# More landing time for the DMAs of two layers in a list-scheduled four-layer graph kernel

## The chip, the cores and the metric

The kernel runs on one core of a Trainium2 chip. The metric is the device time of one execution in microseconds (us). An instruction "record" is one entry of the trace. PE is the matmul engine, PEld its weight load, DVE the vector engine, ACT the scalar engine, POOL GpSimd, and SP the engine that issues nearly all DMAs, from one queue that is worked through in order.

## The reference, cut to what matters

There are 128 graphs of 128 nodes, with 512 features a node, all in fp32. Four different graph layers follow each other, each with a residual and a layer norm.

```python
def reference(x, adj, ...):                       # x (128,128,512), adj (128,128,128)
    # layer 0: attention-like transition, used twice, three weights
    e = leaky_relu(sj[:, None, :] + si[:, :, None] + ab[0])
    alpha = adj * exp(e)
    transition = alpha / (alpha.sum(-1) + 1e-12)
    for k in range(3):
        H = H + Xk @ Wk[k] + bk[k]
        Xk = einsum('bij,bjd->bid', transition, Xk)
    x = layernorm(x + relu(H))
    # layer 1: hypergraph convolution 512 -> 1024 -> 512
    Hm = (adj != 0); w = adj[:, 0, :]             # first row of adj as weights
    conv = lambda x, W, b: Dn * (Hm @ (Be * (Hm^T @ (x @ W^T)))) + b
    y = conv(layer_norm(relu(conv(x, W1, b1))) * gamma + beta, W2, b2)
    x = layernorm(x + (y + x))
    # layer 2: tanh attention over adj; layer 3: 8-head attention, scores scaled by adj + adj
    x = layernorm(x + layer2(x, adj))
    x = layernorm(x + layer3(x, adj))
    return x
```

## The kernel before

The kernel writes no instruction directly. Every operation is first recorded in a `Plan`, with an estimated duration, the operations it depends on and the buffers it needs. A list scheduler (`order`) then plays the whole program through with those estimates, gives each operation a start and each tile a buffer, and `emit` issues the operations in the order of these starts. On the chip each engine takes its instructions strictly in that order and waits at semaphores, so the estimates decide the order and the buffers, and nothing else.

```python
WHEN0 = (-3.0, -1.6, -1.0, 0, 0)                  # when a stage of layer 0 is due, in periods
WHEN1 = (-3.0, -2.3, -1.6, -1.1, .2, .6)          # the same for layer 1; the first entry: its loads
LATENCY = ((0, 205, 215, 255, 300), (225, 120, 110, 200, 200), (160, 145, 140, 200, 200),
           (110, 140, 100, 105, 200), (2300, 2300, 2300, 2300, 2300))   # from engine (row) to engine, ns
ISSUE, BEGIN = 450, 1000
# (cut)
class Plan:
    def add(self, engine, call, name, args, kw):
        moved = 0
        if name == "dma_start":
            run, parts = kw.pop("run", D), kw.pop("parts", P)
            n = next(a for a in args if isinstance(a, View) and a.tile.kind != "dram").idx.size
            moved = 1.1 * parts * max(n // run, 1) * (8 + .038 * 4 * min(run, n)) / 16
        ns = estimate(engine, name, out, rest, kw) * self.share      # ISSUE for a DMA
        if self.group is not None and self.group < len(self.ops):    # "together": one op of several calls
            op = self.ops[self.group]
            op[1].append((call, args, kw)); op[2] += ns; op[7] += moved
        else:
            op = [engine, [(call, args, kw)], ns, (self.key, k), set(), [], shares_port(...), moved]
        # (cut: which earlier operations it depends on)

    def order(self, urgent=None):
        # (cut: ready lists; an operation is picked by rank among those that can start soonest)
            start[k] = t
            free[e] = end = t + o[2]
            if o[7]:                                                 # a DMA: one pipe for all of them
                end = pipe = max(pipe, t + BEGIN) + o[7]
            # (cut)
                    slots[tile.kind].append((end + max(LATENCY[SP if o[7] else e]), place[tile]))
            for j in after[k]:
                come[j] = max(come[j], end + LATENCY[SP if o[7] else e][f])

    def deadlines(self, start):                                      # gives the ranks of a second pass
        # (cut)
                ns, e = (BEGIN + ops[d][7], SP) if ops[d][7] else (ops[d][2], ops[d][0])
                last[d] = min(last[d], by - ns - LATENCY[e][ops[k][0]])
```

Two helpers make groups of small DMAs. `from_dram` loads a tile in blocks that are later turned by the vector engine's 32 by 32 transposes, and `through_dram` writes a tile to device memory and gives back a function that reads it again in another layout.

```python
    def from_dram(src, kind):                     # layer 0: x, as "four"; layer 1: adj, as "sq"
        for j in range(nj):                       # the two graphs of a pair
            with plan.together():
                for k in range(4):
                    sp.dma_start(t[k * Q:(k + 1) * Q, :, j], ..., run=n // 4, parts=Q)   # 32 partitions

    def through_dram(src, name, in_order=True):   # "e" in layer 0, "h" in layer 1, "x" before layer 3
        for j in range(nj):
            with plan.together():
                for m in range(4):
                    sp.dma_start(part(d, ..., j), src[m * Q:(m + 1) * Q, j], run=nw, parts=Q)
        def load(): ...                           # one DMA back
```

Layer 1, for four graphs at a time (its first stages and the hidden layer):

```python
    def layer1(i0):
        loaded = [(load_rows(x1d[i // U]), from_dram(adj[i:i + U], sq)) for i, in each(both)]
        yield                                     # stage 0 above is due at WHEN1[0]
        for (_, ab), in each(loaded):             # stage 1, due at WHEN1[1]
            AT = sq()
            turned(AT, ab)                        # DVE transpose of the adjacency rows
            HT = sq(); cnt = col(U)
            for b in range(U):
                ve.tensor_scalar(HT[:, b], AT[:, b], 0.0, None, op0=OP.not_equal, op1=OP.add, accum_out=...)
        # (cut: HB on POOL, K = H B H^T on PE, x1 K, the left operands of the fast matrix products)
        twice(left, WT["w1"], ...)                # two levels of Strassen: PE into banks, DVE adds
        for r, i in enumerate(both):              # DVE scale and bias, ACT relu and norm, then:
            loads.append(through_dram(h[r][b]..., f"h{i + b}"))
        # (cut: reload h turned, second product, residual, norm, store to x2d)
```

The driver:

```python
    plan.key = -9
    prepare0()
    layer(layer0, 0, WHEN0, size=2)
    # (cut: prepare1, the weights of layer 1)
    layer(layer1, n + LAG1, WHEN1, size=2)
    # (cut: prepare2, prepare_w, prepare3, the weights of layers 2 and 3)
    layer(layer23, 2 * n + LAG1 + LAG2, WHEN2, ramp, size=2)
    plan.emit(places)
```

Of the kernel before, what the change touches and what calls it, by code (L numbers as in the profile page):

```python
# [34 lines left out]

WHEN0 = (-3.0, -1.6, -1.0, 0, 0)
WHENT = (.8, 2.1), (2.0, 3.1)
WHEN1 = (-3.0, -2.3, -1.6, -1.1, .2, .6)
STEP1 = .22
WHENH, WHENW, WHENG = (2.4, 3.0), (2.9, 3.6), (3.6, 4.3)  # L40
WHEN2 = (-2.4, -2.0, -1.45, -1.15, -.7, .3, .5, 2)
WHENV, WHENS, WHENP, WHENO = (.9, 1.9), (2.2, 3.2), (3, 4), (3.5, 4.5)
LAG1, LAG2 = 1, 1.5
SOFT = .2
RAMP = 0, 0, .05, 4

# [10 lines left out]
PE, DVE, ACT, POOL, SP = range(5)  # L57

LATENCY = ((0, 205, 215, 255, 300), (225, 120, 110, 200, 200), (160, 145, 140, 200, 200), (110, 140, 100, 105, 200),
           (2300, 2300, 2300, 2300, 2300))  # L60
# [11 lines left out]
class Tile:  # L72
# [3 lines left out]
    def __init__(self, kind, ap=None):  # L76
        self.kind, self.ap = kind, ap
        self.reads, self.writes = [], []
# [65 lines left out]
def shares_port(engine, name, args, kw):  # L144

    if engine == POOL:
        return name != "memset"
    views = [a for a in args if isinstance(a, View)]
    sbuf = [a for a in views[1:] if a.tile.kind not in PSUM and a.idx.size > 1]
    if engine != DVE or not sbuf:  # L150
        return False
    if name in ("tensor_scalar", "tensor_copy"):
        return "accum_out" not in kw and views[0].idx.size > 1
    return len(sbuf) > 1


def overlap(a, b):

    if a[1] < b[0] or b[1] < a[0]:
        return False  # L160
    if a[3] is None and b[3] is None:
        return True
    one, two = (np.arange(e[0], e[1] + 1) if e[3] is None else e[3] for e in (a, b))
    return np.intersect1d(one, two, assume_unique=True).size > 0


class Plan:


    def __init__(self, slots, later):  # L170
        self.slots = slots
        self.later = later
        self.key = 0
        self.group = None
        self.share = 1
        self.ops = []

    def engine(self, number, real):
# [7 lines left out]
    def add(self, engine, call, name, args, kw):  # L186
        out, rest = args[0], args[1:]
# [5 lines that stand above are left out]
        ns = estimate(engine, name, out, rest, kw) * self.share  # L193
        if self.group is not None and self.group < len(self.ops):
            k = self.group
            op = self.ops[k]
            op[1].append((call, args, kw))
            op[2] += ns
            op[7] += moved
        else:  # L200
            k = len(self.ops)
            op = [engine, [(call, args, kw)], ns, (self.key, k), set(), [], shares_port(engine, name, args, kw), moved]
            self.ops.append(op)
        reads = [a for n, a in [*enumerate(rest), *kw.items()] if isinstance(a, View) and n != "accum_out"]
        writes = [a for a in (out, kw.get("accum_out")) if isinstance(a, View)]
        for v, is_write in [(v, False) for v in reads] + [(v, True) for v in writes]:
            t = v.tile
            if t.kind == "free":
                continue
            if t.kind not in ("fixed", "dram") and t not in op[5]:  # L210
                op[5].append(t)
            lo, hi = int(v.idx.min()), int(v.idx.max())
            whole = v.idx.size > hi - lo
            entry = (lo, hi, k, None if whole else np.unique(v.idx))
            op[4].update(e[2] for e in t.writes if overlap(e, entry))
            if is_write:
                op[4].update(e[2] for e in t.reads if overlap(e, entry))
                if whole:
                    t.reads = [e for e in t.reads if e[0] < lo or e[1] > hi]
                    t.writes = [e for e in t.writes if e[0] < lo or e[1] > hi]  # L220
                t.writes.append(entry)
            else:
                t.reads.append(entry)
        op[4].discard(k)
# [7 lines left out]
    def order(self, urgent=None):  # L232


        ops = self.ops
# [11 lines left out]
        slots = {kind: [(0, i) for i in range(m)] for kind, m in self.slots.items()}  # L247
        place = {}
# [17 lines left out]
        come, free, start = [0.0] * n, [0.0] * 5, [0.0] * n  # L266
# [37 lines left out]
        while count < n:  # L304
            t, e = min((b[0], e) for e, b in enumerate(best) if b)
            k = best[e][1]
            o = ops[k]
            stale = {e}
            for tile in o[5]:
                if tile not in place:  # L310
                    s, l = slots[tile.kind], line[tile.kind]
                    at = min(s)
                    s.remove(at)
                    place[tile] = at[1]
                    l.remove(tile)
                    settle(tile.kind)
                    stale = set(range(5))
            del ready[e][k]
            start[k] = t
            free[e] = end = t + o[2]  # L320
            if o[7]:
                end = pipe = max(pipe, t + BEGIN) + o[7]
            if e == PE and o[3][0] > reached:
                reached = o[3][0]
                stale.add(SP)
            if o[6]:
                port[DVE + POOL - e] = end
                stale.add(DVE + POOL - e)
            count += 1
            for tile in o[5]:  # L330
                todo[tile] -= 1
                if not todo[tile]:
                    slots[tile.kind].append((end + max(LATENCY[SP if o[7] else e]), place[tile]))
                    settle(tile.kind)
                    stale = set(range(5))
            for j in after[k]:
                f = ops[j][0]
                come[j] = max(come[j], end + LATENCY[SP if o[7] else e][f])
                left[j] -= 1
                if not left[j]:  # L340
                    ready[f][j] = come[j]
                    stale.add(f)
            for f in stale:
                best[f] = look(f)
        return start, place, max(free)

    def deadlines(self, start):

        ops = self.ops
        last = [s + 20000 for s in start]  # L350
        for k in sorted(range(len(ops)), key=lambda k: -start[k]):
            for d in ops[k][4]:
                by = start[k] if ops[k][0] == PE else last[k]
                ns, e = (BEGIN + ops[d][7], SP) if ops[d][7] else (ops[d][2], ops[d][0])
                last[d] = min(last[d], by - ns - LATENCY[e][ops[k][0]])
        return last

    def emit(self, places, rounds=2):
# [19 lines left out]
def kernel(  # L378
# [21 lines left out]
    for kind, (n, _) in spans.items():  # L400
        places[kind] = [first[:, at(kind, k):at(kind, k) + SIZE[kind]] for k in range(n)]
        if kind != "w7":
            for k in range(n):
# [3 lines left out]
    slots = {"w7": 7, "out": OUTS, "q7": 0, "q3": 0, "h": 0, "w28": 0, "sq": SQS, "col": COLS, "row": ROWS, "bank": 6, "t0": 1, "t1": 1,  # L407
             "four": BUFS, "row1": 1, "k": KS}
# [16 lines left out]
    plan = Plan(slots, later)  # L425
# [831 lines left out]
    def attention(i0, A, qT, kT, v, x3d, base, r):  # L1257
# [7 lines left out]
        with plan.together(.65):  # L1265
            for b in range(U):
                for i in range(C):
                    for r2 in range(2):
                        pe.matmul(ps[b][r2][:, i * P:(i + 1) * P],
                                  qT[r2 * HD:(r2 + 1) * HD, b, i],  # L1270
                                  kT[r2 * HD:(r2 + 1) * HD, b, i], start=True, stop=True)
        plan.key += SOFT
        for b in range(U):
# [54 lines left out]
    def layer(job, start, when, ramp=lambda k: 0, size=1):  # L1328
        for k in range(0, n, size):
            stages = job(k * U)  # L1330
            for w in when:
                plan.key = start + k + w + ramp(k)
                if start + k + w == when[0]:
                    plan.key = -9.5
                next(stages, None)

    def ramp(k):
        return -RAMP[0] * max(RAMP[1] - k, 0) - RAMP[2] * max(k + RAMP[3] + 1 - n, 0)

    plan.key = -9  # L1340
    prepare0()
    layer(layer0, 0, WHEN0, size=2)
    for job, start, step in ((prepare1, n - 5, .5),):
        plan.key = start
        for k, _ in enumerate(job()):
            plan.key = start + step * (k + 1)
    layer(layer1, n + LAG1, WHEN1, size=2)
    for job, start, step in ((prepare2, 2 * n + LAG1 - .3, .1), (prepare_w, 2 * n + LAG1, 0),
                             (prepare3, 2 * n + LAG1 + 2, .1)):
        plan.key = start  # L1350
        for k, _ in enumerate(job()):
            plan.key = start + step * (k + 1)
    layer(layer23, 2 * n + LAG1 + LAG2, WHEN2, ramp, size=2)
    ctx.enter_context(tc.manual_schedule())
    plan.emit(places)
# [28 lines left out]
```

## Time and profile before

Three runs took 5480.13 us (median; 5480.02 to 5481.23). The profiled execution spans 5477.4 us at a granted matmul clock of 0.994.

| what | value |
|---|---|
| DMA issues of the program | 786374 packets on SP's queue, 759.71 MB |
| mean rate | 140 GB/s, 45.3% of the 16 DMA engines' span |
| x rows of layer 0, 64 KB each | 512 issues, median 2.0 us from issue to landing |
| adjacency rows of layer 1, 16 KB each | 512 issues, median 2.7 us |
| h blocks stored, 128 KB each | 496 issues from one buffer, median 2.4 us |
| h read back, 512 KB each | 87 issues into one kind of buffer, median 4.6 us |

Every operation is recorded by one line of the program (L369), so lines tell nothing here, and groups are told apart by their tiles: `four`, `out`, `first`, `sq`, `col` and `ks` are buffers in the on-chip memory, `bank` and `t` are matmul banks, and `h`, `e`, `x1d`, `x2d` and `K` are scratch in device memory. Layer 0 fills the trace up to about 1300 us, layer 1 from there to about 3100 us, and layers 2 and 3 the rest.

### The profile page before, as it was taken

Reading aid. Unit: us, or ns where it says so; the run is one execution under the profiler, and the core shown is the slowest. Engines: PE = TensorE matmul, PEld = TensorE weight load, DVE = VectorE, ACT = ScalarE, POOL = GpSimd, SP = SyncE. Lnnn points to the kernel's source line nnn. Section 1 sums busy time; section 2 is a strip of 40 time slices with the busy share of each in tenths; the row PEclk is TensorE's granted clock in tenths of the full one; section 3 lists DMA queues with packets and bytes.
Section 4 is the critical chain, followed back from the end, with each engine's and each line's share of the span. In section 5 each row is a group of like instructions: output and inputs, shape, how many; then the busy total and the mean of one; then the engine's idle time right before and its main releaser. Section 6 shows DMA issues by size and latency. Waiting matters only on the chain.

```text
span 5477.4 us, 94041 instructions
## 1 busy us (share of the span) xinstructions
PE 5346.1 (98%) x29145; PEld 4258.7 (78%) x29145; DVE 4549.0 (83%) x11553; ACT 2397.3 (44%) x6479; POOL 4037.1 (74%) x4835
## 2 busy tenths in 40 slices
PE   7999999999999999999999999999999999999998
PEld 4555555555788888888888789899999999999987
DVE  6888887878998899998999978777778777877876
ACT  2444343444443434443434345444455445445444
POOL 6666666666777777777777567777777777777776
PEclk8999999999999999999999999999999999999999
DMA  3333333334554544544454545554454555555553
GB/s 92 98 100 98 104 94 107 93 98 126 153 152 144 155 141 151 155 144 151 149 151 148 161 132 164 160 163 153 161 162 155 162 164 152 161 165 156 161 155 119
DMA packets 788381, 768.35 MB, mean 140 GB/s; under 512 B 264859, under 2 KB 592547, under 8 KB 787878
## 3 DMA queue, kind: packets, MB, share of 16 engines
q1 hardware_dynamic: 786374, 759.71, 45.3%
q8 instruction: 231, 3.78, 0.3%
q10 hardware_dynamic: 1504, 2.62, 0.2%
q14 instruction: 272, 2.23, 0.1%
HBM read 435.83 MB, written 326.24 MB: 139 GB/s over the span
## 4 chain that ended last, share of the span: by engine, by line
PE 56%; DVE 7%; DMA 3%; POOL 2%; issue 1%; ACT 1%; SPq 1%; DVEq 0%; POOLq 0%; ACTq 0%
PE bank L369 42%; PE t L369 14%; DVE first L369 2%; DVE col L369 2%; DVE out L369 1%; DVE four L369 1%; POOL out L369 1%; SPq L369 1%; DMA out<-h 1%; DMA h<-first 1%; DMA out<-x3d 1%; POOL first L369 0%; DMA first<-x3d 0%; ACT first L369 0%; DVE junk L369 0%
## 5 line engine op out<-in xcount | busy, mean ns | idle before, releaser
L369 PE MATMUL bank<-first,four 128*128 128x386 f32 (+3 forms) x5176 | 1438.1, 431 | 32.5 <-DVE out L369 14.2
L369 PEld LDWEIGHTS bank<-first,four 128*128 128x128 f32 (+2 forms) x5176 | 846.3, 187 | 588.6 <-DVE out L369 141.5
L369 DVE TENSOR_TENSOR out<-bank,out 128x386 f32<-128x386 f32 (+1 forms) x1884 | 926.6, 509 | 275.5 <-PE bank L369 215.6
L369 POOL TENSOR_TENSOR out<-out 128x256 f32<-128x256 f32 (+3 forms) x482 | 548.6, 1149 | 297.3 <-DVE out L369 214.0
L369 POOL TENSOR_TENSOR col<-col,neghalf 128x1 f32<-128x1 f32 x640 | 378.8, 597 | 375.6 <-DVE col L369 373.9
L369 DVE TENSOR_TENSOR first<-bank,first 128x256 f32<-128x256 f32 x1362 | 542.1, 412 | 129.6 <-PE bank L369 99.0
L369 PE MATMUL bank<-first,out 128*128 128x256 f32 (+2 forms) x2560 | 623.4, 381 | 25.7 <-DVE first L369 10.1
L369 PEld LDWEIGHTS bank<-first,out 128*128 128x128 f32 (+1 forms) x2560 | 469.4, 190 | 127.3 <-DVE first L369 30.6
L369 PE MATMUL bank<-four,out 128*128 128x256 f32 (+2 forms) x2118 | 538.1, 376 | 2.9 <-DVE col L369 1.4
L369 DVE TENSOR_TENSOR four<-bank,four 128x256 f32<-128x256 f32 x818 | 337.7, 417 | 142.9 <-PE bank L369 128.3
L369 PE MATMUL bank<-out,first 128*128 128x128 f32 (+2 forms) x2840 | 427.8, 290 | 2.2 <-DVE out L369 1.2
L369 ACT COPY out<-bank 128x258 f32<-128x258 f32 (+2 forms) x555 | 236.6, 431 | 419.7 <-PE bank L369 378.6
L369 PEld LDWEIGHTS bank<-four,out 128*128 128x128 f32 (+2 forms) x2118 | 369.7, 189 | 59.1 <-issue 8.4
L369 PEld LDWEIGHTS bank<-out,first 128*128 128x128 f32 (+1 forms) x2840 | 374.4, 188 | 26.0 <-DVE four L369 2.8
L369 ACT ACTIVATE col<-col,col 128x1 f32<-128x1 f32 x640 | 183.2, 292 | 456.2 <-POOL col L369 390.1
L369 POOL TENSOR_TENSOR four<-four,four 128x256 f32<-128x256 f32 (+2 forms) x395 | 329.0, 837 | 13.0 <-DVE four L369 3.2
L369 ACT COPY t<-out 128x512 f32<-128x512 f32 x256 | 150.2, 591 | 421.9 <-DVE four L369 217.6
L369 POOL TENSOR_TENSOR first<-first 128x512 f32<-128x512 f32 (+3 forms) x196 | 232.2, 1197 | 110.3 <-DVE first L369 73.9
L369 POOL TENSOR_TENSOR out<-out,out 128x256 f32<-128x256 f32 (+2 forms) x286 | 288.2, 1011 | 9.3 <-DVE four L369 4.4
L369 POOL TENSOR_TENSOR four<-four 128x256 f32<-128x256 f32 (+2 forms) x331 | 244.3, 754 | 67.6 <-DVE four L369 38.3
L369 POOL TENSOR_SCALAR sq<-sq,col 128x128 f32<-128x128 f32 x256 | 160.5, 636 | 153.4 <-DVE col L369 149.0
L369 DVE BATCH_NORM_STATS2 col<-first 128x6 f32<-128x512 f32 x370 | 245.5, 681 | 27.2 <-ACT first L369 25.4
(406 smaller groups left out, 12715.2 us busy)
## 6 DMA issues: line engine op xcount, KB each, us to landing
h<-first SPq DMA_DIRECT2D x496, 128.0 KB, 2.4
out<-x1d SPq DMA_DIRECT2D x88, 512.0 KB, 4.3
out<-h SPq DMA_DIRECT2D x87, 512.0 KB, 4.6
four<-in_x_dram SPq DMA_DIRECT2D x512, 64.0 KB, 2.0
four<-in_x_dram SPq DMA_DIRECT2D x62, 512.0 KB, 3.5
x1d<-four SPq DMA_DIRECT2D x62, 512.0 KB, 2.7
first<-S SPq DMA_DIRECT2D x61, 512.0 KB, 4.4
out<-S SPq DMA_DIRECT2D x50, 512.0 KB, 4.4
```

What stands on the lines that cost most here:

```text
L369: call(*map(real, args), **{n: real(a) for n, a in kw.items()})
```

## The change

The order is made with longer DMAs. An operation that moves data gets a margin, which is added in the plan to its end: to the time at which its readers can start, and to the time at which its buffers come free. The margin is 1.5 us for what layer 0 records, 3.0 us for what is recorded from layer 1 on up to the weights of layers 2 and 3, and nothing for layers 2 and 3 themselves. Besides, the first stage of layer 1 (x rows and adjacency rows) is due 3.5 periods ahead instead of 3.0. No operation is added or removed, and no duration of a compute operation is changed; order and buffers are what comes out differently.

```diff
-WHEN1 = (-3.0, -2.3, -1.6, -1.1, .2, .6)
+WHEN1 = (-3.5, -2.3, -1.6, -1.1, .2, .6)
+MARGIN = 1500, 3000, 0
...
-            op = [engine, [(call, args, kw)], ns, (self.key, k), set(), [], shares_port(engine, name, args, kw), moved]
+            op = [engine, [(call, args, kw)], ns, (self.key, k), set(), [], shares_port(engine, name, args, kw), moved,
+                  self.margin if moved else 0]
...
-                    slots[tile.kind].append((end + max(LATENCY[SP if o[7] else e]), place[tile]))
+                    slots[tile.kind].append((end + o[8] + max(LATENCY[SP if o[7] else e]), place[tile]))
...
-                come[j] = max(come[j], end + LATENCY[SP if o[7] else e][f])
+                come[j] = max(come[j], end + o[8] + LATENCY[SP if o[7] else e][f])
...
-                last[d] = min(last[d], by - ns - LATENCY[e][ops[k][0]])
+                last[d] = min(last[d], by - ns - ops[d][8] - LATENCY[e][ops[k][0]])
...
+    plan.margin = MARGIN[0]
     layer(layer0, 0, WHEN0, size=2)
...
+    plan.margin = MARGIN[1]
     layer(layer1, n + LAG1, WHEN1, size=2)
...
+    plan.margin = MARGIN[2]
     layer(layer23, 2 * n + LAG1 + LAG2, WHEN2, ramp, size=2)
```

More of the change, by code (lines that the diff above doesn't have):

```diff
@@ L175, in __init__ @@
         self.share = 1
+        self.margin = 0
         self.ops = []
```

## The prediction, made before the changed kernel ran

> **What bounds the kernel now.** I read the busy times of the page first, then a table by stretches, then the waits of one stretch, and last the timeline around one wait.
>
> ```profile
> PE 5346.1 (98%) x29145; PEld 4258.7 (78%) x29145; DVE 4549.0 (83%) x11553; ACT 2397.3 (44%) x6479; POOL 4037.1 (74%) x4835
> ```
>
> PE, the matmul engine, is busy for 98% of the span: 5477.4 - 5346.1 = 131 us are all that is left idle on it. The change adds and removes no matmul, so it can only move these 131 us. Where they lie is seen in the table by stretches (borders in us, length, busy us and records of each engine, granted clock, share of the DMA engines, GB/s):
>
> ```profile
> 0.00:137.00 137.00, 108.12 (x315) 60.65 (x316) 92.48 (x178) 38.00 (x87) 90.59 (x105) 0.89 0.34 92
> 137.00:1150.00 1013.00, 1009.54 (x3003) 544.02 (x3001) 824.38 (x2112) 415.97 (x967) 682.03 (x814) 1.00 0.34 100
> 1150.00:1450.00 300.00, 276.38 (x1004) 171.92 (x1003) 254.73 (x639) 121.17 (x266) 202.08 (x247) 0.98 0.40 118
> 1450.00:3100.00 1650.00, 1620.85 (x7735) 1363.18 (x7734) 1493.65 (x3698) 673.27 (x1269) 1272.99 (x1482) 1.00 0.50 151
> 3100.00:3300.00 200.00, 180.51 (x1118) 156.23 (x1116) 162.90 (x395) 76.66 (x228) 119.23 (x145) 0.97 0.46 142
> 3300.00:5300.00 2000.00, 1994.59 (x14830) 1822.44 (x14829) 1597.30 (x4237) 987.91 (x3366) 1550.89 (x1912) 1.00 0.51 160
> 5300.00:5477.00 177.00, 156.10 (x1153) 140.25 (x1151) 123.57 (x301) 84.31 (x298) 119.30 (x135) 0.96 0.39 127
> ```
>
> Length minus the first busy figure is PE's idle time: 28.9 us in the start, 3.5 in layer 0, 23.6 where layer 0 passes into layer 1, 29.2 in layer 1, 19.5 where layers 2 and 3 begin, 5.4 in them, 20.9 in the tail. Layer 0 is full. Layer 1 is the one steady stretch with something to gain, and there DVE is busy for 1493.65 of 1650 us, 91%, so a DVE that is held up for a microsecond soon holds up PE.
>
> What PE waits for in layer 1 (total us, times, longest), and then DVE's waits for DMAs in the same stretch:
>
> ```profile
> PE bank L369 <- DVE col L369: 10.4, 11, 1.8
> PE bank L369 <- DVE first L369: 7.5, 17, 1.0
> PE t L369 <- DVE col L369: 3.6, 3, 1.8
> PE t L369 <- DVE first L369: 2.7, 7, 0.7
> ```
>
> ```profile
> DVE sq L369 <- DMA sq<-in_adj_dram: 8.6, 9, 1.4
> DVE out L369 <- DMA out<-x1d: 0.3, 1, 0.3
> ```
>
> PE waits for DVE, not for a DMA. DVE waits for one kind of DMA, the adjacency rows, nine times, 8.6 us in all. The timeline shows one of the nine from the issue to the damage: first SP's queue, then DVE, then PE.
>
> ```profile
> 1845.64 0.44 SPq L369 DMA_DIRECT2D out<-h  x1
> 1846.14 5.38 SPq L369 DMA_DIRECT2D sq<-in_adj_dram  x8
> ```
>
> ```profile
> 1851.64 0.17 DVE L369 BATCH_NORM_AGGREGATE col<-col 128x2 f32<-128x6 f32 x1
> 1853.21 0.45 DVE L369 STREAM_TRANSPOSE sq<-sq 128x256 f32<-128x256 f32 x1 [1.39 <-DMA sq<-in_adj_dram]
> ```
>
> ```profile
> 1854.02 0.70 PE L369 MATMUL t<-first,out 128*128 128x256 f32 x2 [1.13 <-DVE col L369]
> ```
>
> The eight small DMAs of one pair take SP 5.38 us to issue, behind a 512 KB reload of h. They are there at 1853.2, 7.1 us after the first issue. DVE stands for 1.39 us at the transpose, in front of the additions that free the banks, and PE stands for 1.13 us. The wait names the statistics (col) as PE's releaser; the root is the DMA.
>
> **What the Trainium skill says.** The page "DMA: Bandwidth & Descriptors", section "Anatomy of one DMA — SWDGE (gpsimd) path", says that DMA engines do not wait on semaphores and that any wait happens on the issuing sequencer before dispatch. The trace agrees for SP's queue too: in layer 1 it stands 571.8 us in 120 waits for ACT's results in the buffer `first` (the h that is stored), and all that stands behind is issued later. "Perfetto Trace Analysis", section "Per-instruction lifecycle: what the profiler-reported window actually captures", says that the window of a DMA on the issuing engine leaves out the movement of the data. It agrees: an adjacency DMA shows a median of 0.43 us on SP and lands 2.8 us after its issue. "Rules for kernel authors" of the DMA page advises to issue early and to wait late, which is what a margin asks of the order; that it helps here no run has shown yet. "Identifying the Most-Contended Engine" of the trace page warns that matmul busy time says little of the distance to the roofline. That is so, but PE's pace when it is not idle is constant here (243 records in each 50 us of layer 1 that is full), so that its idle time does say what a new order can win.
>
> **The change part by part.**
>
> (1) Adjacency rows of layer 1. The old plan takes a group of four such DMAs as 0.45 us of issue each and lets the data flow from 1.0 us after the group's start: 1.1 x 32 x 4 x (8 + .038 x 128) / 16 = 113 ns each, 0.9 us for eight, then 2.3 us latency. That is 4.2 us from the start to the transpose. In the trace eight issues alone take 8 x 0.43 = 3.4 us (5.38 in the case above) and the last lands at least 1.5 us, at the median 2.8 us later: 4.9 to 8.2 us. The plan is thus 1 to 4 us short, and the margin of 3.0 us makes it 7.2 us. Listing both programs in their order of issue, I counted the matmul calls between the start of a group of these loads and the transpose that reads them: before, 9 at least, 10 at the tenth percentile, 15 at the median; after, 13, 29 and 55. A call is two records, 50 us / 121.5 = 0.41 us. (Of the 40 calls more, the start half a period sooner is most: 64 pairs in 1300 to 3100 us make 28 us a period, half of it 14 us or 34 calls; the margin's 3 us are 7.) So the distance goes from 3.7, 4.1 and 6.2 us to 5.3, 12 and 23 us. All but the very nearest loads land well in time, and most of the 8.6 us of DVE waits must go. On PE, the gaps that follow these transposes directly are 1.03, 1.13, 0.87, 0.69, 0.46, 0.33, 1.06 and 0.37 us, in sum 5.9 us. Gain: 6 us.
>
> (2) The round trip of h. The reload is issued 16 calls after the store at the median before (least 0) and 21 after (least 16). A stored block lands 2.4 us after its issue (the median), and the DMAs of h take 6.5 us at the longest; 16 calls are 6.6 us. Where the reload came too early, SP stood before it: 12.7 us in 18 waits for h<-first. These go. SP is not the bound; what stands behind it comes a little sooner. I give it 1 us.
>
> (3) Layer 0. x rows: 32 calls ahead before, 31 after. The reload of e after its store: 8 calls, then 10, at 50 us / 75 = 0.67 us per call. DVE's waits for x (7.2 us) and e (4.9 us) shrink, but PE is idle for 3.5 us of 1013 in all. Gain: 0.
>
> (4) The rest of layer 1 is dealt anew. 23 us of its idle are not behind late rows. Four gaps of 1.77 to 1.84 us come every 438 us, at 1618, 2059, 2497 and 2936 us, where DVE's 128x1024 scaling takes 2.28 us once and normalisations crowd in front of a bank's release. Only about 55% of PE's instructions and 27% of DVE's keep their successor in layer 1, so such patterns break and others come. I take -2 us, give or take 10.
>
> (5) The two passages, 23.6 and 19.5 us idle, are reordered as well (45% of PE's successors stay): -3 us, give or take 8.
>
> (6) Layers 2 and 3. Their margin is nothing, and 99% of PE's instructions keep their successor. Gain: 0. The start keeps its 28.9 us within a few microseconds.
>
> Sum: -6 - 1 - 0 - 2 - 3 - 0 = -12 us, 5480 - 12 = 5468 us.
>
> **The rivals.** (A) The wait is only renamed. DVE is at 91% in layer 1, and if PE's gaps come from DVE's load, removing 8.6 us of DVE waits lets it reach the next crowded spot with the same lag. For it: the larger gaps (1.8 us) have no DMA behind them. Against it: DVE still has 150 us of slack there, and the gap shown above opens with the transpose. Time: 5476 to 5481. (B) The plan now holds each buffer for 1.5 or 3 us longer than needed, so it packs tighter elsewhere. For it: operands that POOL makes within 8 calls of their matmul go from 28 to 56 in layer 1, and those of ACT within 4 calls from 280 to 417 in layer 0. New small waits of PE for POOL and ACT would cost 5 to 15 us: 5485 to 5495. Against it: operands that DVE makes within 2 calls fall, 894 to 829 in layer 0 and 635 to 612 in layer 1. (C) All goes well: the late rows, the repeated gaps and a third of the passages go, 6 + 7 + 14 us: about 5453. (D) The rows come earlier and meet the 512 KB reloads, and the DMA engines slow down. At a mean share of 0.50 in layer 1 there is room; I give it little.
>
> **Range and chances.** The 72 us of idle in layer 1 and the two passages bound the gain; it would take 110 us for 2%. A loss of 2% would need the idle of layer 1 to grow almost fivefold. The spread of (4) and (5) is about 13 us together, so the range is 5450 to 5488 us. Within 2%: 0.98, the rest split evenly. That it is faster at all I hold for likely, about seven in ten.
>
> **What would show it.** DVE's waits for adjacency rows in layer 1 below 2 us instead of 8.6 confirm (1); PE idle there near 20 us instead of 29 confirms (1), (2) and (4). Layer 0 at over 99% PE confirms (3); a stretch with more than 6 us of new PE waits for ACT or POOL there would be rival (B). Layers 2 and 3 must be alike in length within 2 us. The prediction is wrong if the adjacency waits vanish and layer 1 keeps its 29 us (A), if the passages change by more than 15 us, or if DMA landing times in layer 1 grow (D).

## The result and the profile after

The changed kernel takes 5494.32 us (median of 4 runs, 5493.05 to 5495.52) against 5480.08 us before: ratio 1.0026, 95% interval 1.0009 to 1.0044. It is slower by 14 us, where 12 us less were predicted. PE is busy for 5346.1 us in both profiles, so what the change cost is idle time of PE: 131.3 us before, 146.2 us after.

The table by stretches of the changed kernel, with the same columns as the one shown of before (borders, length, busy us and records of PE, PEld, DVE, ACT and POOL, clock, DMA share, GB/s):

```profile
137.00:1150.00 1013.00, 1008.59 (x3009) 550.35 (x3008) 827.18 (x2112) 415.48 (x967) 683.66 (x816) 1.00 0.35 100
1150.00:1450.00 300.00, 274.89 (x1005) 170.78 (x1004) 255.08 (x649) 123.05 (x268) 206.86 (x248) 0.98 0.42 122
1450.00:3100.00 1650.00, 1612.33 (x7676) 1353.51 (x7675) 1499.89 (x3667) 672.02 (x1261) 1271.19 (x1478) 1.00 0.50 150
3100.00:3300.00 200.00, 177.81 (x1077) 154.48 (x1076) 161.70 (x381) 75.06 (x224) 116.85 (x136) 0.96 0.45 136
3300.00:5300.00 2000.00, 1991.91 (x14793) 1820.23 (x14792) 1601.03 (x4239) 991.38 (x3361) 1551.69 (x1910) 1.00 0.51 160
```

PE is idle for 37.7 us of 1450 to 3100 us, where it was 29.2, and does 59 records less in them. Layer 0 stays full. What PE waits for in layer 1, and what DVE waits for from DMAs there (total us, times, longest):

```profile
PE bank L372 <- DVE first L372: 12.5, 24, 0.9
PE bank L372 <- DVE out L372: 5.2, 4, 1.8
PE bank L372 <- ACT out L372: 4.8, 5, 1.5
PE bank L372 <- DVE junk L372: 3.0, 2, 2.6
```

```profile
DVE sq L372 <- DMA ks<-K: 0.2, 1, 0.2
DVE sq L372 <- DMA out<-h: 0.2, 1, 0.2
```

The nine waits for adjacency rows are gone, as meant: 8.9 us of DVE's waits for DMAs became 0.4 (the two that are left are put down to a DMA that landed at that time). The gaps that were put down to `col` are gone with them. Waits for other results of DVE and for ACT stand in their place, and they are longer in sum (36.3 us against 28.6).

To see where the time goes in spite of work that shifts across fixed borders, I cut each trace at four stores: the issue of the 60th store to x1d (end of layer 0), of the 60th to x2d (end of layer 1), of the 4th and of the 58th to the output. Lengths and PE's idle time in us, from one profile each:

| part | before | after | difference | PE idle before | PE idle after |
|---|---|---|---|---|---|
| up to the 60th store of x1d | 1297.7 | 1291.7 | -6.0 | 38.3 | 36.0 |
| to the 60th store of x2d | 1769.1 | 1774.8 | +5.7 | 45.9 | 52.9 |
| to the 4th store of the output (the passage) | 328.0 | 339.4 | +11.4 | 20.4 | 27.4 |
| to the 58th (layers 2 and 3) | 1923.3 | 1925.1 | +1.8 | 5.4 | 7.8 |
| to the end | 159.3 | 161.4 | +2.1 | 21.3 | 22.2 |

Of the nine kernels below whose layer 0 stands in exactly the order of before, eight differ from it by up to 2.1 us at the first cut and one by 5.1 us, so a single part says little under about 5 us. The passage stands out in length. Its lines, before and then after:

```profile
3066.80:3394.80 328.00, 307.55 (x1964) 269.29 (x1963) 269.46 (x671) 139.29 (x426) 208.20 (x249) 0.98 0.50 157
3066.50:3405.90 339.40, 312.04 (x1979) 273.38 (x1978) 276.98 (x678) 140.81 (x426) 212.55 (x252) 0.97 0.49 151
```

Only 7.0 of its 11.4 us are idle time of PE. In the other 4.4 us PE is busy: it does 15 records more there, at a slightly lower granted clock (0.97, 0.98 before). The part that holds layer 1 does 18 records less, and so its length hides that its idle time grew by 7.0 us as well.

The two longest gaps of the passage in the changed kernel, first PE, then DVE in front of them:

```profile
3136.01 0.48 PE L372 MATMUL bank<-ident,col 128*128 128x128 f32 x1 [6.17 <-DVE junk L372]
...
3157.32 3.78 PE L372 MATMUL bank<-sq,four 128*128 128x128 f32 x16 [7.40 <-DVE sq L372]
```

```profile
3122.82 8.98 DVE L372 TENSOR_TENSOR first<-first 128x256 f32<-128x256 f32 x9
...
3135.27 0.68 DVE L372 SCALAR_TENSOR_TENSOR junk<-four,row 128x512 f32<-128x512 f32 x1
...
3156.82 0.45 DVE L372 STREAM_TRANSPOSE sq<-sq 128x256 f32<-128x256 f32 x1 [5.90 <-DMA sq<-F]
```

DVE combines the weights of layer 3 for 9 us in one go (first<-first, nine instructions), and the dot products with which layer 2 begins (junk) come after it. PE has nothing else left and stands for 6.17 us. The 9 us are not all work. Four of the nine instructions overlap additions of 128x512 on POOL and take 5.74 us; six of the same shape in the kernel before, while POOL stands, take 2.10 us:

```profile
3123.13 5.74 DVE L372 TENSOR_TENSOR first<-first 128x256 f32<-128x256 f32 x4
3123.10 2.10 DVE L369 TENSOR_TENSOR first<-first 128x256 f32<-128x256 f32 x6
```

At the pace of the second line the four would take 1.4 us, so by estimate 4.3 of the 6.17 us come from the overlap.

The second gap is layer 2's round trip of F through device memory, which nothing covers: DVE waits 5.90 us for it. A lower clock goes with this gap: the granted clock is 1.00 from 3149 to 3152 us, and 0.50 from 3153 to 3161 us. So PE takes 3.78 us for the 16 matmuls of the line above; in the kernel before, 16 of the same shape followed a short gap at a clock of 1.00 and took 2.05 us:

```profile
3141.47 2.05 PE L369 MATMUL bank<-sq,four 128*128 128x128 f32 x16 [0.61 <-DVE sq L369]
```

In the kernel before, DVE's stretch was dealt the other way round:

```profile
3121.69 0.67 DVE L369 SCALAR_TENSOR_TENSOR junk<-four,row 128x512 f32<-128x512 f32 x1
...
3123.10 4.03 DVE L369 TENSOR_TENSOR first<-first 128x256 f32<-128x256 f32 x7
```

Here the first dots stand before the combinations. PE's longest gap was 4.65 us (at 3130 us).

### The profile page after: what moved, and what is told of

Same layout as the page of the kernel before. It is cut to its first block, busy times and chain, and to the rows that moved or that the text cites. A ratio compares the mean times of both kernels' runs of the same rounds, so it can differ in the third digit from the quotient of the medians.

```text
span 5492.3 us, 94146 instructions
## 1 busy us (share of the span) xinstructions
PE 5346.1 (97%) x29145; PEld 4263.9 (78%) x29145; DVE 4570.5 (83%) x11553; ACT 2406.0 (44%) x6479; POOL 4046.9 (74%) x4835
## 3 DMA queue, kind: packets, MB, share of 16 engines
q8 instruction: 231, 3.78, 0.3%
## 4 chain that ended last, share of the span: by engine, by line
PE 80%; DVE 12%; DMA 2%; issue 2%; ACT 2%; POOL 1%; SPq 1%; DVEq 0%; POOLq 0%; ACTq 0%
PE bank L372 62%; PE t L372 18%; DVE out L372 4%; DVE first L372 3%; DVE col L372 2%; DVE four L372 2%; SPq L372 1%; ACT first L372 1%; POOL out L372 1%; ACT out L372 1%; DVE junk L372 0%; DVE sq L372 0%; DMA four<-in_x_dram 0%; DMA ks<-x3d 0%; DMA sq<-F 0%
## 5 line engine op out<-in xcount | busy, mean ns | idle before, releaser
L372 PE MATMUL bank<-first,out 128*128 128x256 f32 (+3 forms) x2894 | 707.2, 380 | 25.5 <-DVE first L372 12.2
L372 PEld LDWEIGHTS bank<-first,out 128*128 128x128 f32 (+2 forms) x2894 | 519.3, 189 | 141.4 <-DVE first L372 30.6
L372 DVE TENSOR_TENSOR first<-bank,first 128x256 f32<-128x256 f32 x1161 | 466.4, 416 | 88.7 <-PE bank L372 53.2
L372 DVE TENSOR_TENSOR four<-bank,four 128x256 f32<-128x256 f32 x952 | 390.4, 418 | 148.4 <-PE bank L372 131.4
L372 PE MATMUL bank<-four,out 128*128 128x256 f32 (+1 forms) x1504 | 406.5, 378 | 1.6 <-DVE first L372 0.9
L372 POOL TENSOR_TENSOR four<-four,four 128x256 f32<-128x256 f32 (+2 forms) x463 | 383.7, 833 | 10.7 <-DVE four L372 3.0
L372 PE MATMUL bank<-out,four 128*128 128x256 f32 (+2 forms) x1756 | 310.5, 335 | 0.7 <-DVE four L372 0.6
L372 PEld LDWEIGHTS bank<-four,out 128*128 128x128 f32 (+1 forms) x1504 | 276.7, 189 | 42.4 <-issue 2.9
L372 PE MATMUL bank<-four,first 128*128 128x128 f32 (+3 forms) x1976 | 293.8, 289 | 0.2
L372 PEld LDWEIGHTS bank<-four,first 128*128 128x128 f32 (+2 forms) x1976 | 254.0, 187 | 15.6 <-DVE four L372 2.0
```

Of the source, the lines that this page charges most:

```text
L372: call(*map(real, args), **{n: real(a) for n, a in kw.items()})
```

## The experiments

Every run is compared with the kernel before in the same set; its median lay between 5477.6 and 5484.5 us from set to set, so ratios count, not times across sets. Three theories were open: M (the margins as such), E (the early loads), L (a lottery of orders).

**The halves of the change.** `-3.0` stands for WHEN1[0] as before.

```diff
-WHEN1[0] = -3.5, MARGIN = 1500, 3000, 0      # the changed kernel
+WHEN1[0] = -3.0, MARGIN = 1500, 3000, 0      # e1
+WHEN1[0] = -3.5, MARGIN = 0, 0, 0            # e2
+WHEN1[0] = -3.0, MARGIN = 1500, 0, 0         # e3
+WHEN1[0] = -3.0, MARGIN = 0, 3000, 0         # e4
```

> Both margins as in the change, layer 1's loads due at -3.0 periods as before. Theory M (the margins make an order in which DVE and POOL get in each other's way): 5490 to 5498 us, as the whole change. Theory E (the loads due half a period sooner do it, by holding the adjacency buffers longer): the margins alone keep their gain, 5465 to 5478 us. Theory L (a lottery: any nudge of the plan deals the order of layer 1 and the passages anew, and the time follows no rule): anything from 5465 to 5505 us, unlike the whole change.

> Loads due at -3.5 periods, no margin. Theory E: 5490 to 5498 us. Theory M: 5472 to 5482 us, as before. Theory L: anything from 5465 to 5505 us. Under all three DVE's 8.6 us of waits for adjacency rows should shrink to under 3 us, as the rows are issued sooner by about 14 us.

> Only the margin of 1.5 us in layer 0. Theory M with its weight on layer 1: within 3 us of before, 5477 to 5483 us, as layer 0 is 99.6% PE in both. If the passage into layer 1 or the order after it is reshuffled by it (theory L), up to 15 us either way, with PE's idle time growing or shrinking after 1150 us.

> Only the margin of 3.0 us from layer 1 on, loads due at -3.0. Theory M: nearly the whole loss, 5488 to 5497 us, with DVE's mean time per instruction in layer 1 near 409 ns as after the change (404 before). Theory E: 5465 to 5478 us. Theory L: anything from 5465 to 5505 us.

Measured: both margins 5506.58 us, ratio 1.0038 (1.0023 to 1.0053); early loads 0.9999 (0.9990 to 1.0008); layer 0's margin 1.0004 (0.9995 to 1.0013); layer 1's margin 0.9999 (0.9990 to 1.0007). No part alone costs anything, and the two margins together cost 24 us by the medians. So the effects do not add, which neither M nor E allows. In e1's profile PE is idle for 141.7 us, 10.4 more than before, and also busy for 5363.9 us, 17.8 more, over the same 29145 records; why it is busy longer stays open. The prediction held that part fixed. The cuts showed that e4 is 20 us ahead of before at the end of layer 1, and loses it all behind: 11.8 us in the passage, and 12 us in layers 2 and 3, which the margin doesn't touch. In e1, e2 and e4 alike those layers took 1932 to 1935 us instead of 1923. The cause lies in `emit`, as f4 below shows: it makes one order, improves it twice by deadlines, and keeps an improvement if the plan holds it shorter. Before and after keep the first one, e1, e2 and e4 the second, in which only 75% of PE's instructions of layers 2 and 3 have the successor they had.

**The margin cut to size.**

```diff
 layer(layer1, n + LAG1, WHEN1, size=2)
+plan.margin = 0                              # e7 (else the whole change), e10 (else e4)
-loaded = [(load_rows(x1d[i // U]), from_dram(adj[i:i + U], sq)) for i, in each(both)]
+x1 = load_rows(x1d[i // U])                  # e8: -3.0, no other margin
+plan.margin = 3000
+loaded.append((x1, from_dram(adj[i:i + U], sq)))
+plan.margin = 0
+WHEN1[0] = -3.0, MARGIN = 0, 100, 0          # e5
```

> The whole change, but the margin ends with layer 1, so that the weights of layers 2 and 3 are recorded without it. In the changed kernel all of the loss lies behind the 60th store of layer 1: from there to the fourth store of the last layer it takes 339.4 us instead of 328.0, as in every kernel so far with the 3 us margin. Theory W (the margin on the weights' loads delays the passage): 328 to 332 us there and 5481 to 5486 us in all. Theory R (layer 1's own end, or the reshuffled order of the passage, costs it): still 336 us or more there, 5488 to 5496 us in all.

> Margin of 3.0 us in layer 1 only, not on the weights after it, loads due at -3.0. Layer 0 and layer 1 as with the margin from layer 1 on (60th store of layer 1 at 3047 us, 20 us before the kernel before). Theory W: passage 328 to 332 us, total 5466 to 5471 us. Theory R: passage near 340 us and total near 5479 us. Layers 2 and 3 stand in the second of two orders here, which took 1932 to 1935 us three times, against 1921 to 1925 us for the order of before; so 1930 us or more there under both.

> Margin of 3.0 us on the adjacency loads of layer 1 alone, due at -3.0; layer 0, and layers 2 and 3, stand in the order of before. If the late rows are what layer 1 loses (the prediction's step 1): DVE's waits for them below 1 us, PE's idle in layer 1 down by about 6 us, 5470 to 5476 us. If the order of DVE and POOL sets it (any new order deals new gaps): waits gone all the same, and the time anywhere from 5472 to 5490 us.

> A margin of 0.1 us from layer 1 on: far too little to cover a late row, but enough to deal layer 1 anew (a third to two thirds of the instructions keep their successor); layer 0, and layers 2 and 3, stand in the order of before. Theory L: moves the time of layer 1 by 5 to 15 us, in either direction, as the real margin does. If the order of layer 1 matters only through its waits for DMAs: within 3 us of before, 5477 to 5483 us.

Measured: e7 1.0013 (1.0004 to 1.0022), passage 336.8 us; e10 1.0005 (0.9997 to 1.0014), passage 344.3 us. Ending the margin before the weights does not bring the passage back, so theory W falls there; e7's whole time, 5485.88 us, lies in W's range all the same, and e10's does not. e8 is 6.4 us faster, 0.9989 (0.9980 to 0.9997), with DVE waiting 1.2 us for DMAs in layer 1 and PE idle for 21.8 us of it instead of 27.0. This agrees with the 6 us of step (1), but it does not isolate them: e8 deals layer 1 anew too (62% of PE's operations and 30% of DVE's keep their successor there, by the two plans). e5 is the surprise: 5462.42 us, 0.9970 (0.9960 to 0.9980), the fastest kernel of the study, with a margin far too small to cover a late row, and about as much of layer 1 dealt anew (64% and 31%). DVE still waits for rows in it, and yet PE is idle for 14.2 us of layer 1 instead of 27.0. The waits, and the stretch between the 4th and the 60th store of x2d, of e5, then that of before:

```profile
DVE sq L372 <- DMA sq<-in_adj_dram: 3.4, 4, 1.1
```

```profile
1531.40:3058.00 1526.60, 1512.39 (x7198) 1266.08 (x7197) 1376.88 (x3425) 625.80 (x1172) 1221.21 (x1391) 1.00 0.49 149
```

```profile
1531.80:3066.80 1535.00, 1507.99 (x7200) 1269.10 (x7199) 1387.72 (x3425) 624.93 (x1172) 1196.16 (x1392) 1.00 0.49 149
```

The same 3425 DVE records take 1376.88 us in e5 and 1387.72 before. DVE's waits for DMAs fell by about 4 us (8.9 to 4.7), PE's idle time by 12.8: most of what e5 gains in layer 1 comes from its order, not from data that landed sooner.

**One improvement for all.** The number of improvements is held fixed.

```diff
-def emit(self, places, rounds=2):
+def emit(self, places, rounds=1):            # f1 (else e2), f2 (else e4), f3 (else e1)
-            if other[2] < end:
+            if True:                         # f4 (else the kernel before)
```

> The plan makes one order and two improvements of it, and keeps an improvement if the plan holds it better. The kernel before and the changed one keep the first improvement; so do the runs with the margin on layer 0 alone, on the adjacency rows alone, and of 0.1 us. Margins only, early loads only and both runs with 3 us in layer 1 keep the second, and in all of these layers 2 and 3 take 1932 to 1935 us instead of 1919 to 1928. This run: early loads only, held to the first improvement. Theory P (which improvement is kept sets layers 2 and 3): 1919 to 1926 us there. If the early loads are what costs the changed kernel its 14 us: 5488 to 5496 us. If they cost nothing in layer 1: 5475 to 5483 us.

> Margin of 3.0 us from layer 1 on, loads due at -3.0, held to the first improvement. Theory P: layers 2 and 3 at 1919 to 1926 us, so about 10 us less there than the same margin took with the second (1935 us). If the margin gains in layer 1 what the waits cost: 5466 to 5474 us. If the large margin costs in the passage, as in the three runs with it (339 to 340 us against 328): 5476 to 5484 us.

> Both margins, loads due at -3.0, held to the first improvement: the changed kernel without its early loads. If the early loads cost the 14 us: 5474 to 5484 us. If the two margins do: 5490 to 5498 us. With the second improvement the same margins took 5507 us; theory P gives back about 10 us of that and no more (5494 to 5499 us), a reshuffle theory anything.

> The kernel before with no margin and no early loads, but the second improvement kept. Theory P: layers 2 and 3 take 1930 to 1936 us instead of 1923, though nothing is changed in the plan's numbers; layer 1 in the range of the others with the second (60th store of layer 1 at 3047 to 3076 us), the whole 5478 to 5492 us. If not the improvement but the margins or the early loads set layers 2 and 3: 1919 to 1926 us.

Measured: f1 1.0002 (0.9994 to 1.0011); f2 1.0030 (1.0019 to 1.0041); f3 1.0009 (1.0000 to 1.0018); f4 1.0006 (0.9997 to 1.0014). f4 has no margin at all, and layers 2 and 3 take 1939.1 us in it: theory P holds for what the second improvement costs there, 9 to 16 us in five kernels of five. It fails in f2, which keeps the first and takes 1931 us. Layer 1's margin that was free with the second improvement costs 16 us with the first (f2), and 5 us once layer 0 has its margin too (f3). f4 shows one more thing. Its layer 1 has more waits for late rows than any other:

```profile
DVE sq L369 <- DMA sq<-in_adj_dram: 17.1, 17, 1.6
```

```profile
1528.10:3065.40 1537.30, 1510.47 (x7211) 1270.93 (x7210) 1373.39 (x3428) 626.19 (x1173) 1204.33 (x1392) 1.00 0.50 148
```

PE is idle for 26.8 us there, the same as before (27.0), with twice the waits for rows. DVE stands at more DMAs and has less to do meanwhile (1373 us). So the sum of DVE's waits for rows does not say how long PE idles.

**The residual beside POOL.** Among DVE's groups one changed its duration between the 4th store of x2d and the 4th of the output: scalar_tensor_tensor of 128x512 on two buffers, the residual of layer 1. Its largest rows (count, busy us, mean ns), before and then after; the row with a matmul bank among its operands is for comparison:

```profile
L369 DVE SCALAR_TENSOR_TENSOR out<-rows,col 128x512 f32<-128x512 f32 x76 | 61.3, 824 | 0.0
L369 DVE SCALAR_TENSOR_TENSOR out<-bank,col,out 128x512 f32<-128x512 f32 x61 | 44.5, 735 | 0.3
```

```profile
L372 DVE SCALAR_TENSOR_TENSOR out<-rows,col 128x512 f32<-128x512 f32 x80 | 80.1, 1007 | 0.0
L372 DVE SCALAR_TENSOR_TENSOR out<-bank,col,out 128x512 f32<-128x512 f32 x62 | 45.7, 742 | 4.9 <-PE bank L372 4.1
```

Over all its rows the group went from 233.4 to 262.0 us (x266, 877 to 985 ns). The Trainium skill's page "SBUF — State Buffer", section "Who interferes with whom", says that a DVE instruction with two inputs in the on-chip memory contends with a GpSimd instruction that reads it. The rows agree as to which are stretched: 824 to 1007 ns with two buffers, 735 to 742 with a bank. The traces also agree as to when. Between the same stores 60 instructions of the group overlapped no POOL instruction before and took 702 ns on average, and the 206 that did took 938; after, it is 39 at 700 ns and 227 at 1039. Whether the stretch makes the time was tried with the reloads that feed the residual:

```diff
+plan.margin = 0                              # h1 (else f2); h2: 3000
 x1 = load_rows(x1d[i // U])                  # the last stage of layer 1
 K = tile_of("k", U, M)
 sp.dma_start(K.rearrange("p b n -> p (b n)"), kept[r], run=U * M)
+plan.margin = MARGIN[1]                      # h1; h2: 0, and MARGIN = 0, 0, 0
```

> Margin of 3.0 us from layer 1 on, first improvement kept, but no margin on the reloads of x1 and K in the last stage of layer 1 (with it: 5501 us, 984 ns). Theory Q (the margin on these reloads moves the residual of layer 1 beside POOL's work, and DVE is stretched): the residual's instructions back to 870 to 900 ns, time back to 5468 to 5482 us. Theory L (any order with a large margin, or any new order, may stretch them): still above 930 ns and 5488 us or more, or no relation of the two.

> The reverse: margin of 3.0 us on the reloads of x1 and K of layer 1 alone. Theory Q: the residual's instructions at 950 to 990 ns and 5488 to 5502 us. If the reloads are not it: 870 to 900 ns and 5470 to 5482 us.

Measured: h1 1.0010 (1.0003 to 1.0016), 916 ns; h2 1.0000 (0.9991 to 1.0009), 930 ns. Taking the margin off these reloads gives back two thirds of f2's loss, but putting it on alone costs nothing, and in h2 the group is stretched without a loss. Theory Q is not borne out for these reloads: the stretch goes along with a new order, and 930 ns cost nothing. That 985 ns cost nothing in the changed kernel is not shown; there the same kind of overlap, on the weights, stands in front of PE's gap of 6.17 us.

**Sizes of the margin, and the better part of both.**

```diff
-MARGIN = 0, 100, 0                           # e5
+MARGIN = 0, 50, 0                            # g_50; g_400: 400, g_1000: 1000
+MARGIN = 1500, 100, 0                        # h4
```

> Margin of 1.0 us from layer 1 on (first improvement is kept). If the loss grows with the margin: between 5462 us (0.1 us) and 5501 us (3 us), about 5475, with the residual's instructions at 890 to 930 ns. Theory L: anything from 5460 to 5505 us, and no relation of margin and time; a time above 5490 us or below 5465 us would speak for it.

> Margin of 1.5 us in layer 0, as in the change, and 0.1 us from layer 1 on, loads due at -3.0. If the gains add: 5456 to 5461 us. If layer 0's margin only moves its stores and gains nothing by the end, as alone (ratio 1.0004): 5462 to 5467 us. Theory L (layer 1 is dealt anew after the new layer 0): anything from 5460 to 5495 us.

> Margin of 0.05 us from layer 1 on; no late row can be covered by it. A rule that grows with the margin puts it at or below the ratio of 0.1 us (0.997 or a little under, 5460 to 5466 us) or between that and 1. Theory L: unrelated to 0.1 us although twice as near to it as to any other, anywhere from 0.997 to 1.003. DVE's waits for DMAs in layer 1 stay at 4 us or more under both.

> Margin of 0.4 us from layer 1 on. A rule that grows with the margin puts it between 0.1 us (0.997) and 1.0 us (1.003): 0.998 to 1.002. Theory L: anywhere from 0.997 to 1.003, and outside of that band if it is dealt badly or well.

Measured, all with the first improvement (layer 0's margin 0 except in the last row):

| margin from layer 1 on, us | ratio | DVE's waits for DMAs in layer 1, us | passage against before, us |
|---|---|---|---|
| 0.05 | 0.9994 (0.9986 to 1.0003) | 5.4 | -0.8 |
| 0.1 | 0.9970 (0.9960 to 0.9980) | 4.7 | -6.5 |
| 0.4 | 0.9990 (0.9981 to 0.9998) | 0.3 | +6.0 |
| 1.0 | 1.0030 (1.0019 to 1.0041) | 1.3 | +16.4 |
| 3.0 (f2) | 1.0030 (1.0019 to 1.0041) | 0.2 | +6.2 |
| 0.1, with 1.5 in layer 0 (h4) | 0.9982 (0.9973 to 0.9990) | 6.1 | -8.0 |

DVE's waits fall once the margin reaches 0.4 us, and the time does not follow them: the two fastest still have 5 to 6 us of waits. 0.05 and 0.4 us fell into the band that a rule allowed, but it is no proof of one, since f2 and f3, both at 3 us (f3 with layer 0's margin besides), differ by 0.2%. h4 did not add layer 0's gain: it is 5.7 us ahead at the end of layer 0 (the margin there is worth 4.5 to 6.0 us up to that cut in the five kernels that have it with the first improvement), and 2.6 us of this are lost up to the end of layer 1; e3 loses 9.6. Layer 0's gain is given back in the passage into layer 1.

The passage into layer 2 is the one thing that goes with the edits. It is longer by 6.0 to 16.4 us in all twelve kernels that put 0.4 us or more on layer 1's DMAs at large or load early (the changed kernel, f1, f2, f3, h1, g_400, g_1000, e1, e2, e4, e7, e10), and between 8.0 us shorter and 2.6 us longer in the seven without (e3, e5, e8, g_50, h2, h4, f4). The two groups were formed after the results, and in PE's idle time they part less clearly: 0.1 to 10.0 us more in the twelve, from 4.1 less to 2.7 more in the seven. The uncovered round trip of F is not what the twelve share: DVE waits for no F in the passages of e1, e4, e7 and g_1000, which are 8.8 to 16.4 us longer.

**What the plan held of itself.** The third value that `order` returns is the planned end of the program, and the code of each kernel gives it without a chip. (The plan's order is the one that ran: the loads and stores of `sq` stand at its places among the 4150 DMA issues of SP in all twenty traces.) The plan before ends at 5359.0 us, that of the changed kernel at 5368.9. So the plan itself became 9.9 us longer, and the kernel 14. Over the nineteen kernels that were compared with the one before the planned end and the measured ratio go together (correlation 0.73): e1 is 13.1 us longer than before in the plan, f2 11.9, and e5 5.5 us shorter. It misses some: g_1000 is 2.4 us longer in the plan and 16 on the chip, f3 14.8 and 5. The planned end counts the margins as if the data came that late, so it does not prove a cause; but the outcomes are less of a lottery than theory L has them.

## Why the prediction was wrong

- **Step (1), late rows: the waits went as foretold, the gain is not isolated.** Predicted 6 us; e8, which puts the margin on these loads alone, gained 6.4 us, but with a new order in layer 1. The step's sum has a slip: the plan starts the second group of four DMAs 1.8 us after the first, so it allowed 1.8 + 1.0 + 0.45 + 2.3 = 5.55 us up to the transpose, not 4.2, and 8.55 with the margin. The plan was at most 2.7 us short of the 8.2 us read from the trace, not 4.
- **Step (2), the round trip of h: mis-sized.** SP's waits for h<-first were to go; they are 12.6 us in 18 waits after (12.7 in 18 before). It was given 1 us; it is nothing.
- **Step (3), layer 0: right for the whole.** Ratio 1.0004 with this margin alone. The 6 us that are won by its end are lost in front of layer 1.
- **Step (4), the rest of layer 1: wrong in sign, and the term that failed most.** Predicted -2 us, give or take 10; steps (1), (2) and (4) together were to bring PE's idle time from 1450 to 3100 us from 29.2 to near 20 us. It rose to 37.7, by 8.5 us, although the waits for rows were gone. If those were worth their 6 us, the new deal cost about 14 us there. The prediction took a new order of a nearly full stage for even-handed; the runs show that the order alone moves PE's idle time there, to 14.2 us in e5 and 33.0 in g_1000 (27.0 before, between the stores of x2d).
- **Step (5), the passages: wrong in sign too.** Predicted -3 us, give or take 8. Between the prediction's borders the two have 4.2 us more idle time, between the stores 8.3 (1.3 from the 60th of x1d to the 4th of x2d, and 7.0 in the passage into layer 2), and the passage into layer 2 is 11.4 us longer. Its two gaps show how in this kernel: weights combined ahead of the dots and stretched beside POOL, an uncovered round trip, and a lower clock behind it. Large margins or early loads lengthened it twelve times of twelve; by what common way is not known.
- **Step (6): nearly right** for this pair, +1.8 us, since both kept the first improvement. That layers 2 and 3 hang on that choice was missed. It did not decide here, but hid what e4 had gained up to the end of layer 1.
- **Rivals.** Rival (B) had the right range (5485 to 5495 us) and part of the reason: waits of PE for ACT in layer 1 grew (2.8 to 8.2 us), but those for POOL hardly (0.6 to 0.9 us), and layer 0 gained none. Rival (A) is right in one sense: the waits vanish and the idle time stays. The test named for it, 29 us that stay, was exceeded (37.7 us). Rival (D)'s sign was there, without a cost that shows: in layer 1 the 512 KB reads landed later (out<-h 5.1 us after issue instead of 4.6, out<-x1d 4.8 instead of 4.2), the adjacency rows sooner (1.9 instead of 2.8), and DVE waited for DMAs 0.4 us in all. Nothing of rival (C) came.

Open: why the passage grows with these edits, and what in e5's order is better. A profile was taken once for each kernel (e5's in its slowest run, 5469.43 us), so the parts of a few microseconds are not sure.

## What to carry to other kernels

When a scheduler's estimates are edited, the whole order is dealt anew, and at 98% PE this can outweigh the wait that was to be removed: 0.05 to 3 us of margin moved this kernel between -0.3% and +0.4%, with no relation to the waits that were left. So put a correction on the one estimate that is wrong (here the grouped adjacency loads), see first whether the plan's own end grows, and compare several nearby values by measurement before a cause is named. Look at where stages meet, and at any choice among whole orders, before crediting a steady stage with the result.

## What was not expected of the hardware

DVE's waits for DMAs were no measure of the time: 25.8 us of them in layer 1 (f4) and 0.2 us (f2) went with stretches of 1537 and 1538 us. Instructions with two operands in the on-chip buffers stretched by 12% on average by order alone (877 to 985 ns), as more of them fell beside a POOL instruction and each took longer there (206 at 938 ns before, 227 at 1039 after; about 700 ns where none overlapped), while those with a bank operand kept to within 1% (735 and 742 ns). And during a gap of PE of 7.40 us the granted clock fell from 1.00 to 0.50, at which the next 16 matmuls took 3.78 us instead of 2.05.
